# Slice attention of a four-layer graph model: softmax rows kept, turned later inside the slice mixing, and one product moved to another engine

## The chip, the cores and the metric

The kernel runs on one core of one Trainium2 chip. The core has a matrix engine (TensorE; PE in the profile, its weight loads PEld), three elementwise engines (VectorE: DVE, ScalarE: ACT, GpSimd: POOL) and a queue processor (SyncE: SP) that here mostly starts DMA transfers. Each engine takes its own instructions in the order of its queue, and waits on semaphores for the others. On-chip memory is SBUF (128 partitions); matrix products land in PSUM, which has eight banks.

The metric is the device time of the whole kernel in microseconds (us). Times are medians of several runs.

## The reference

A model of four layers works on N = 2708 nodes with D = 256 features and an adjacency matrix; each layer is a graph stage ("gnn") and a token stage ("ffn"), both with a residual. The change is in the token stage of layer 0, attention over 64 learned slices with 8 heads of 64:

```python
fx = (x @ W_fx.T + b_fx).reshape(B, N, H, P).transpose(0, 2, 1, 3)
xm = (x @ W_x.T + b_x).reshape(B, N, H, P).transpose(0, 2, 1, 3)
temp = jnp.maximum(temperature, 1e-06)
sw = jax.nn.softmax((xm @ W_slice.T + b_slice) / temp, axis=-1)
snorm = sw.sum(2)
st = jnp.einsum('bhnc,bhng->bhgc', fx, sw) / (snorm + 1e-05)[..., None]
...
ot = _hydra(st, hy_in_w, hy_conv_w, hy_conv_b, ...)
ot = ot.reshape(B, G, H, P).transpose(0, 2, 1, 3)
out = jnp.einsum('bhgc,bhng->bhnc', ot, sw).transpose(0, 2, 1, 3).reshape(B, N, D_INNER)
return out @ out_w.T + out_b
```

So every node gets, for each head, a softmax over 64 slices (512 weights in all); the weights pool the nodes into 64 slice tokens of 512 features; `_hydra`, a small state-space block run forwards and backwards, mixes the 64 tokens; and the same weights spread the result back over the nodes. The layer after it begins with `x + (concat(a @ x / deg, x) @ weight + bias)` on the layer-normed x ("L1 gnn").

## The kernel before

The 2708 rows are 22 tiles: 21 of 128 rows and a last one of 20. All is 32-bit float here. The stage has three parts, in `fast_l0_ffn`.

**The loop over the 22 tiles.** For each tile TensorE computes 512 logits (L2355: four instructions of the machine in two products of 128 input features, into `lg_ps`). VectorE adds a bias (L2367), takes the maximum per head (L2368) and subtracts it (L2369); ScalarE takes the exponential (L2372); VectorE sums per head (L2373), takes the reciprocal (L2374) and multiplies (L2375). The result `sw` (128 x 512, three buffers) then goes twice through TensorE: as the weights of the slice sums `T` (L2381, four blocks of 128 slices, accumulated over all tiles, 257 columns: the 256 normed features `fa` and a column of ones), and through four 128 x 128 transposes (L2388) into a PSUM tile that ScalarE copies (L2389) to `swT` (128 x 4 x 2708). GpSimd meanwhile adds the output bias to the residual rows (L2363, x + ob), which nothing in this loop waits for; before it, GpSimd scales an output weight of the mixing block by the norm weight (L1968, four products of 128 x 512, on data from a DMA). After the last tile, VectorE divides the sums by their weights (`Tn`).

**`Slices.mix`**, the mixing block: a long chain of small products on TensorE with elementwise work between them on the other engines, from `Tn` to `Z` (128 x 4 x 256: the mixed slices times the output projection). Its PSUM tiles a_ps to g_ps take seven banks.

**The output product.** For each tile four products of `swT` (as weights) with `Z` (L2402) and an addition to x (L2410).

The normed rows `fa`, their transposes `fT` and the projection weights lie in pools of `Pooling` that were opened before the graph stage of layer 0, in an `ExitStack` named `c0` which is closed after the ffn. What comes after is laid into the memory that becomes free then: the constants and expert weights of layer 1's routing (`Route`), and `fa`, `w`, `b` and `V` of `fast_l1_gnn`, whose front norms all rows (L1652, L1654), transposes them, projects them (L2440, into `v_ps`), splits the product into three 16-bit parts (L2451 to L2454; GpSimd makes the last) and adds the bias (L2456, GpSimd) and the own part (L2457) to x. Then comes its long loop over the adjacency matrix (L2511).

The order in each queue is not that of the source: a scheduler lays out the instructions of all engines ahead of time from its own estimates, pool by pool, so that instructions of neighbouring stages and tiles are interleaved. An instruction that reuses a buffer waits for the last reader of what lay there.

Of the kernel before, what the change touches and what calls it, by code (L numbers as in the profile page):

```python
# [18 lines left out]
N = 2708  # L19
# [1893 lines left out]
class Slices:  # L1913
# [59 lines left out]
            )  # L1973
        self.ob = ob

    def mix(self, Tn, Z):

        k, pool = self.k, self.pool
        nc, tc = k.nc, k.tc
# [3 lines left out]
        with tc.tile_pool(name="ps_b0h", bufs=1, space=PSUM) as ps, tc.tile_pool(  # L1983
# [3 lines left out]
            def psum(shape, tag):  # L1987
                return ps.tile(shape, F32, name=tag)

            def new(name, shape):  # L1990
                return sb.tile(shape, F32, name=name)


            TT = new("TT", [128, 2, DI])
            snr = new("snr", [1, DI])
            for kk in range(2):
                p_ = psum([128, DI], ("a_ps", "b_ps")[kk])
                for q in range(4):
                    nc.tensor.transpose(
                        p_[:, q * 128 : (q + 1) * 128],  # L2000
                        Tn[:, q, kk * 128 : (kk + 1) * 128],
                        ident,
                    )
                k.copy(TT[:, kk, :], p_)
            p_ = psum([1, DI], "c_ps")
            for q in range(4):
                nc.tensor.transpose(
# [21 lines left out]
            def in_proj_T(pt, c0, nch):  # L2029

                for kk in range(4):
# [5 lines left out]
                        stop=(kk == 3),  # L2037
                    )


            pd = psum([16, 64], "e_ps")
            in_proj_T(pd, 1152, 16)
# [3 lines left out]
            pb = psum([64, 2, 64], "b_ps")  # L2046
            for m in range(2):
                in_proj_T(pb[:, m, :], 2 * DI + m * 64, 64)
            t16, e16, a1, a2, dt = (new(n, [16, 64]) for n in ("t16", "e16", "a1", "a2", "dt"))
            v.tensor_scalar(t16, pd, self.dtb, None, ALU.add)  # L2050
            v.scalar_tensor_tensor(e16, t16, -1.0, t16, ALU.mult, ALU.max)
# [33 lines left out]
            xc = new("xc", [128, 6, 64])  # L2085
            nc.scalar.activation(xc, ca, AF.Silu)


            cT = new("cT", [64, 3, 16])
            pt = psum([64, 3, 16], "f_ps")  # L2090
# [5 lines left out]
            for back in range(2):  # L2096
                pr = psum([64, H, 64], ("c_ps", "d_ps")[back])
                crow = cum[:, 0:64] if back else cum[:, 1:65]
                hs = slice(back * H, (back + 1) * H)
                for h in range(H):  # L2100
                    c = back * H + h
                    nc.tensor.matmul(
                        pr[:, h, :],
                        lhsT=ident[0:16, c : c + 1].to_broadcast([16, 64]),
                        rhs=crow,
                        start=True,
                        stop=True,
                    )
                col = cT[:, 1 + back, hs, None].to_broadcast([64, H, 64])
                if back:  # L2110
                    v.tensor_tensor(E[1], col, pr, ALU.subtract)
                else:
                    v.tensor_tensor(E[0], pr, col, ALU.subtract)
                v.tensor_scalar(E[back], E[back], 0.0, None, ALU.min)
                nc.scalar.activation(E[back], E[back], AF.Exp)

            pg = psum([64, 64], "e_ps")
            nc.tensor.matmul(pg, lhsT=xc[:64, 4, :], rhs=xc[:64, 5, :], start=True, stop=True)
# [41 lines left out]
                )  # L2160
            zs = new("zs", [64, DI])
            nc.scalar.activation(zs, pz, AF.Silu)
            xr = new("xr", [64, H, P])
            pt = psum([64, DI], "a_ps")
            for q in range(4):
# [18 lines left out]
                )  # L2184
            v.tensor_tensor(y3, y3, py, ALU.add)
            v.tensor_tensor(yg, yg, zs, ALU.mult)

            ms = new("ms", [64, 1])
            nc.scalar.activation(zs, yg, AF.Square, accum_out=ms)
# [11 lines left out]
            for q in range(4):  # L2201
                for kk in range(4):
                    nc.tensor.matmul(
                        po[:, q, :],
                        lhsT=self.wo[:, kk, q * 128 : (q + 1) * 128],
                        rhs=ygT[:, kk, :],
                        start=(kk == 0),
                        stop=(kk == 3),
                    )
            bd = new("bd", [128, 4, 128])  # L2210
            nc.gpsimd.memset(bd, 0.0)
            v.tensor_copy(bd[0:64, :, 0:64], po[0:64])
# [2 lines left out]
            for s in range(2):  # L2215
                nc.tensor.matmul(
                    pm[s * 64 : s * 64 + 64],
                    lhsT=ident[:64, :64],
                    rhs=ms,
                    start=True,  # L2220
                    stop=True,
                )
            m2 = new("m2", [128, 1])
            v.tensor_copy(m2, pm)
            for q in range(4):
# [10 lines left out]
class Pooling:  # L2236
# [3 lines left out]
    def __init__(self, k, w, ctx):  # L2240
        self.k, self.w = k, w
        tc = k.tc
        H, G = 8, 64
        DI = H * G
        pool = ctx.enter_context(tc.tile_pool(name="b0a", bufs=1))
        self.tmp = ctx.enter_context(tc.tile_pool(name="b0n", bufs=2))
        self.fa = pool.tile([128, NT, D + 1], F32, name="fa")
        self.fT = pool.tile([128, 2, N], F32, name="fT")
        self.wc = pool.tile([128, 2, DI], F32, name="wc")
        self.bw = pool.tile([128, DI], F32, name="bw")  # L2250
        k.nc.gpsimd.memset(self.fa[:, :, D : D + 1], 1.0)
# [69 lines left out]
        yield  # L2321


def fast_l0_ffn(k, w, front):

# [3 lines left out]
    DI = H * P  # L2331
    with ExitStack() as ctx:
        keep = ctx.enter_context(tc.tile_pool(name="b0", bufs=1))
        swT = keep.tile([128, 4, N], F32, name="swT")
        Tn = keep.tile([128, 4, D + 1], F32, name="Tn")
        Z = keep.tile([128, 4, D], F32, name="Z")
        slices = Slices(k, w, ctx)
# [2 lines left out]
        with tc.tile_pool(name="b0t", bufs=3) as tmp:  # L2340
            with tc.tile_pool(name="ps_b0l", bufs=2, space=PSUM) as psl, tc.tile_pool(
                name="ps_b0T", bufs=1, space=PSUM
            ) as psT:

                def psum():
                    return psl.tile([128, 512], F32, name="swt_ps")

                side = front.chunk(*CHUNKS[-1], psum)
                T = [psT.tile([128, D + 1], F32, name=f"T{q}_ps") for q in range(4)]
                for t in range(NT):  # L2350
                    p = sz(t)
                    next(side, None)
                    lg = psl.tile([128, DI], F32, name="lg_ps")
                    for kk in range(2):
                        nc.tensor.matmul(  # L2355
                            lg[:p],
                            lhsT=fT[:, kk, t * 128 : t * 128 + p],
                            rhs=wc[:, kk, :],
                            start=(kk == 0),
                            stop=(kk == 1),  # L2360
                        )
                    xt = k.x[:p, t, :]
                    nc.gpsimd.tensor_tensor(xt, xt, slices.ob[:p], ALU.add)  # L2363
                    sw = tmp.tile([128, DI], F32, name="sw")
                    mx = tmp.tile([128, H], F32, name="mx")
                    s3 = sw[:p].rearrange("p (h g) -> p h g", h=H)
                    nc.vector.tensor_tensor(sw[:p], lg[:p], bw[:p], ALU.add)  # L2367
                    nc.vector.tensor_reduce(mx[:p], s3, AX.X, ALU.max)  # L2368
                    nc.vector.tensor_tensor(  # L2369
                        s3, s3, mx[:p, :, None].to_broadcast([p, H, G]), ALU.subtract  # L2370
                    )
                    nc.scalar.activation(sw[:p], sw[:p], AF.Exp)  # L2372
                    nc.vector.tensor_reduce(mx[:p], s3, AX.X, ALU.add)  # L2373
                    nc.vector.reciprocal(mx[:p], mx[:p])  # L2374
                    nc.vector.tensor_tensor(  # L2375
                        s3, s3, mx[:p, :, None].to_broadcast([p, H, G]), ALU.mult
                    )
                    tp = psum().rearrange("p (q n) -> p q n", q=4)
                    for q in range(4):
                        cols = slice(q * 128, (q + 1) * 128)  # L2380
                        nc.tensor.matmul(  # L2381
                            T[q],
                            lhsT=sw[:p, cols],
                            rhs=fa[:p, t, :],
                            start=(t == 0),
                            stop=(t == NT - 1),
                        )
                        nc.tensor.transpose(tp[:, q, :p], sw[:p, cols], ident[:p, :p])  # L2388
                    nc.scalar.copy(swT[:, :, t * 128 : t * 128 + p], tp[:, :, :p])  # L2389
                for q in range(4):  # L2390
                    sc = tmp.tile([128, 1], F32, name="sc")
                    nc.vector.tensor_scalar(sc, T[q][:, D : D + 1], 1e-5, None, ALU.add)
                    nc.vector.reciprocal(sc, sc)
                    nc.vector.tensor_scalar(Tn[:, q, :], T[q], sc, None, ALU.mult)

        slices.mix(Tn, Z)
        with tc.tile_pool(name="ps_b0o", bufs=3, space=PSUM) as ps:
            for t in range(NT):
                p = sz(t)
# [2145 lines left out]
def model(tc, I, out):  # L4545
# [4 lines left out]
    with tc.tile_pool(name="flags", bufs=1) as fp:  # L4550
# [4 lines left out]
        with ExitStack() as ctx:  # L4555
            k = Fast(ctx, tc, I["x"], bad, adjT)
            with tc.tile_pool(name="lists", bufs=1) as lp:
                edges = Edges(k, part(I, "L2_ffn_"), lp)
                with ExitStack() as c0:
# [1 line left out]
                    fast_l0_gnn(  # L4561
                        k, adjT, I["L0_gnn_WqkT"], pooling, edges.search(range(4), "right")
                    )
                    fast_l0_ffn(k, part(I, "L0_ffn_"), pooling)
                order = (0, 1, 5, 2, 3, 4)
                with ExitStack() as c1:
                    route = Route(k, c1, part(I, "L1_ffn_"), 16)
# [131 lines left out]
```

## Time and profile before

| what | value |
|---|---|
| median of 3 runs | 2408.55 us (2408.13 to 2414.51) |
| profiled execution, its own time | 2408.92 us |
| its span, first to last instruction | 2407.1 us |
| mean granted TensorE clock | 0.961 |
| softmax loop, first L2367 to last `Tn` | 372.8 to 468.6 us |
| `mix`, first transpose to first output product | 468.7 to 520.6 us |
| output product | 520.6 to 561.4 us |
| front of layer 1's graph stage | 561.4 to 613 us |

The profile is one execution. Engine rows give busy time, share of the span and number of instructions. The chain of work that ended last is, by share of the span:

```
PE 27%; DVE 3%; issue 1%; DMA 0%; POOL 0%; ACT 0%; POOLq 0%; DVEq 0%; ACTq 0%
```

In forty equal slices of the span, tenths of busy time and of the TensorE clock that was granted (the slice attention lies in slices 7 to 10, counted from one):

```
PE   7999999989899899999799999999999999969997
DVE  7588888645676558456655563234499998853544
PEclk9999999869999999999899997899999999979998
```

In all views used below, a row names the line of the kernel, the engine, the operation, and the tiles as "out<-in"; `[3.49 <-PE lg_ps L2355]` means that the engine was idle for 3.49 us before the instruction and that the PE instruction on that line ended the wait.

### The profile page before, as it was taken

What the parts mean: (1) busy time and instruction counts of PE and PEld (TensorE: products, weight loads), DVE (VectorE), ACT (ScalarE), POOL (GpSimd) and SP (SyncE); (2) the same over time, 40 slices, a digit from 0 to 9 for tenths busy, and PEclk for the clock granted to TensorE, in tenths of its full rate; (3) what the DMA queues carried; (4) which work ended last, traced back from release to release, by engine and by line L of the source; (5) the groups of instructions that cost most, each with busy time, mean ns of one, the idle gap of its engine ahead of it and who ended that gap; (6) DMA issues with size and microseconds to landing.
All of it is one profiled execution on the core that took longest, in us unless ns stands there. A gap on an engine that the chain in (4) does not pass through costs nothing. (4 is left out here: it accounts for less than half of the span.)

```text
span 2407.1 us, 31811 instructions
## 1 busy us (share of the span) xinstructions
PE 2263.5 (94%) x11620; PEld 1501.1 (62%) x11620; DVE 1530.9 (64%) x3386; ACT 687.1 (29%) x1388; POOL 454.6 (19%) x496
## 2 busy tenths in 40 slices
PE   7999999989899899999799999999999999969997
PEld 4777765577778676777578877666632333325664
DVE  7588888645676558456655563234499998853544
ACT  6433333213655222212230013233411112111121
POOL 1100013004100243565130002510030000002221
PEclk9999999869999999999899997999999999979998
DMA  5244322200756244332345523000033433314430
GB/s 150 66 114 115 113 79 79 72 4 12 236 176 188 62 116 96 82 77 48 78 135 150 146 67 59 21 1 18 1 85 101 117 108 110 92 55 160 130 123 15
DMA packets 158572, 219.99 MB, mean 91 GB/s; under 512 B 30911, under 2 KB 94115, under 8 KB 158404
## 3 DMA queue, kind: packets, MB, share of 16 engines
q1 hardware_dynamic: 126096, 179.84, 25.7%
q0 software_dynamic: 15488, 24.04, 4.9%
q10 hardware_dynamic: 16820, 13.95, 1.8%
q8 instruction: 95, 1.56, 0.3%
q14 instruction: 73, 0.60, 0.1%
HBM read 193.49 MB, written 24.82 MB: 91 GB/s over the span
## 5 line engine op out<-in xcount | busy, mean ns | idle before, releaser
L3548 DVE SCALAR_TENSOR_TENSOR PT<-Rr,Q,aj 128x512 f32<-128x512 f32 (+3 forms) x630 | 412.5, 708 | 95.8 <-PE acc_ps L3643 73.9
L3716 PE MATMUL acc_ps<-PT,V 128*64 128x512 f32 (+4 forms) x2016 | 338.9, 551 | 0.7 <-DVE PT L3548 0.2
L3716 PEld LDWEIGHTS acc_ps<-PT,V 128*64 128x64 f32 (+1 forms) x2016 | 95.3, 123 | 215.3 <-issue 163.1
L1844 PE MATMUL acc_ps<-fa,PT 128*128 128x257 f32 x882 | 215.4, 383 | 1.2 <-DVE out L1864 1.2
L1844 PEld LDWEIGHTS acc_ps<-fa,PT 128*128 128x128 f32 x882 | 163.9, 190 | 66.5 <-issue 33.8
L3643 PE MATMUL acc_ps<-V,PT 128*128 128x257 f32 x882 | 194.7, 381 | 1.0 <-POOL V L3511 0.9
L3643 PEld LDWEIGHTS acc_ps<-V,PT 128*128 128x128 f32 x882 | 166.1, 190 | 28.8 <-POOL V L3511 1.2
L3304 PE MATMUL h_ps<-xT,w1t 128*128 128x384 f32 x512 | 176.6, 498 | 3.7 <-ACT xT L3295 3.7
L3321 PE MATMUL y_ps<-w2t,hT 128*128 128x256 f32 x768 | 169.8, 380 | 0.0
L2511 PE MATMUL acc_ps<-V,at 128*128 128x257 bf16 x1323 | 157.1, 277 | 9.8 <-DVE at L2502 7.9
L3321 PEld LDWEIGHTS y_ps<-w2t,hT 128*128 128x128 f32 x768 | 144.9, 190 | 21.1
L2511 PEld LDWEIGHTS <-at 128*128 128x128 bf16 x1323 | 129.0, 99 | 32.9 <-DVE at L2502 5.5
L3304 PEld LDWEIGHTS h_ps<-xT,w1t 128*128 128x128 f32 x512 | 95.6, 192 | 67.9 <-ACT xT L3295 8.3
L1816 ACT ACTIVATE PT<-s_ps,rq 128x512 f32<-128x512 f32 (+1 forms) x126 | 79.5, 636 | 174.4 <-PE s_ps L1792 168.8
L3333 POOL DMA_INDIRECT acc<-ys,ids x48 | 92.0, 1916 | 154.1 <-DVE ys L3330 145.3
L4064 PE MATMUL y_ps<-w2t,hT 128*128 128x256 f32 (+1 forms) x528 | 119.9, 379 | 0.3 <-ACT hT L4057 0.3
L1792 PE MATMUL s_ps<-KT,QT 128*128 128x512 f32 (+1 forms) x252 | 116.2, 548 | 2.5 <-ACT PT L1816 1.6
L4050 PE MATMUL h_ps<-fT,w1t 128*128 128x512 f32 (+1 forms) x288 | 116.0, 552 | 1.9 <-PEq L4110 1.9
L3003 POOL DMA_INDIRECT xe<-fd,idg x48 | 79.6, 1659 | 195.1 <-DVE early_f L3034 180.8
L1817 DVE SCALAR_TENSOR_TENSOR PT<-aj,PT 128x512 f32<-128x512 int32 (+1 forms) x126 | 79.2, 633 | 57.9 <-ACT PT L1816 57.5
L4495 PE MATMUL y_ps<-w2t,hT 128*128 128x256 f32 (+1 forms) x512 | 112.8, 380 | 0.0
L4064 PEld LDWEIGHTS y_ps<-w2t,hT 128*128 128x128 f32 (+1 forms) x528 | 97.1, 186 | 21.3 <-issue 6.9
(745 smaller groups left out, 3368.8 us busy)
## 6 DMA issues: line engine op xcount, KB each, us to landing
aj<-in_adjT SPq DMA_DIRECT2D x399, 256.0 KB, 2.8
w1t<-in_L_ffn_W SPq DMA_DIRECT2D x8, 1024.0 KB
w2t<-in_L_ffn_W SPq DMA_DIRECT2D x8, 1024.0 KB
w1t<-in_L_ffn_w SPq DMA_DIRECT2D x8, 1024.0 KB, 5.6
w2t<-in_L_ffn_w SPq DMA_DIRECT2D x8, 1024.0 KB
aj<-in_adjT SPq DMA_DIRECT2D x63, 74.0 KB, 2.1
fd<-fa ACTq DMA_DIRECT2D x9, 512.0 KB, 3.1
aj<-in_adjT SPq DMA_DIRECT2D x21, 202.0 KB, 2.4
```

Source lines behind the costliest of these rows:

```text
L1792: nc.tensor.matmul(s[:, :cs], lhsT=QT[:, j * 128 : j * 128 + 128], rhs=KT[:, c0 : c0 + cs], start=True, stop=True,)
L1844: nc.tensor.matmul(ac, lhsT=PT[:, o : o + n], rhs=fa[:, j, :], start=j == 0, stop=False)
L2511: nc.tensor.matmul(ac[:, c:], lhsT=at[:, o : o + n], rhs=V[:, j, r], start=j == 0 and q == 0, stop=False, skip_group_check=True,)
L3304: nc.tensor.matmul(hp, lhsT=w1t[:, kk, m * 128 : (m + 1) * 128], rhs=self.xT[:, kk, :], start=(kk == 0), stop=(kk == 1),)
L3321: nc.tensor.matmul(y, lhsT=self.hT[:, m, i * 128 : (i + 1) * 128], rhs=w2t[:, m, :], start=(m == 0), stop=(m == M - 1),)
L3333: add = nc.gpsimd.indirect_dma_start(out=acc, out_offset=bass.IndirectOffsetOnAxis(ap=self.ids[:, i : i + 1], axis=0), in_=ys, in_offset=None,
L3548: nc.vector.scalar_tensor_tensor(PT, R, Q, aj, ALU.max, ALU.mult)
L3643: nc.tensor.matmul(ac[:n], lhsT=PT[:, o : o + n], rhs=V[:, j, 0, :], start=(j == 0), stop=False,)
L3716: nc.tensor.matmul(w.pop("out"), **w)
L4050: nc.tensor.matmul(o[:, :cs], lhsT=w1t[:, kk, m * 128 : (m + 1) * 128], rhs=fT[:, kk, c0 : c0 + cs], start=(kk == 0), stop=(kk == 1),)
L4064: nc.tensor.matmul(y[:n], lhsT=hT[:, m, o : o + n], rhs=w2t[:, m, :], start=(m == 0), stop=(m == M - 1),)
L4495: nc.tensor.matmul(y[:n], lhsT=hT[:, m, o : o + n], rhs=w2t[:, m, :], start=(m == 0), stop=(m == M - 1),)
```

## The change

Four things are done together.

1. The softmax rows of all tiles are kept, in `sws` (128 x 22 x 512), in the pool where `swT` was. The four transposes and the copy of each tile go out of the loop.
2. The last multiply of the softmax goes from VectorE to GpSimd.
3. The pools of `Pooling` are opened on the other side of memory, and `done()`, which is `c0.close`, gives them up after the loop, before `mix`. `swT` is laid out there.
4. A generator `turn()` makes the transposes (through one PSUM bank, `swt_ps`) and the copy of one tile at a time, every third on VectorE and the others on ScalarE. `mix` advances it at nine places with `fill(n)`, 21 tiles in all; the rest is done after `mix`. The output product is as before.

```diff
-    def mix(self, Tn, Z):
+    def mix(self, Tn, Z, side):
+            def fill(n):
+                for _ in range(n):
+                    next(side, None)
...
@@ Pooling.__init__
-        pool = ctx.enter_context(tc.tile_pool(name="b0a", bufs=1))
-        self.tmp = ctx.enter_context(tc.tile_pool(name="b0n", bufs=2))
+        right = dict(side="right")
+        pool = ctx.enter_context(tc.tile_pool(name="b0a", bufs=1, **right))
+        self.tmp = ctx.enter_context(tc.tile_pool(name="b0n", bufs=2, **right))
...
@@ fast_l0_ffn
-        swT = keep.tile([128, 4, N], F32, name="swT")
+        sws = keep.tile([128, NT, DI], F32, name="sws")
...
-                    sw = tmp.tile([128, DI], F32, name="sw")
+                    sw = sws[:, t, :]
...
-                    nc.vector.tensor_tensor(
+                    nc.gpsimd.tensor_tensor(
                         s3, s3, mx[:p, :, None].to_broadcast([p, H, G]), ALU.mult
                     )
-                    tp = psum().rearrange("p (q n) -> p q n", q=4)
                     for q in range(4):
...
-                        nc.tensor.transpose(tp[:, q, :p], sw[:p, cols], ident[:p, :p])
-                    nc.scalar.copy(swT[:, :, t * 128 : t * 128 + p], tp[:, :, :p])
...
-        slices.mix(Tn, Z)
+        done()
+        late = ctx.enter_context(tc.tile_pool(name="b0s", bufs=1, side="right"))
+        swT = late.tile([128, 4, N], F32, name="swT")
+        with tc.tile_pool(name="ps_b0s", bufs=1, space=PSUM, side="right") as ps:
+            def turn():
+                for t in range(NT):
+                    p = sz(t)
+                    tp = ps.tile([128, 4, 128], F32, name="swt_ps")
+                    for q in range(4):
+                        nc.tensor.transpose(
+                            tp[:, q, :p], sws[:p, t, q * 128 : (q + 1) * 128], ident[:p, :p]
+                        )
+                    (nc.vector.tensor_copy if t % 3 == 2 else nc.scalar.copy)(
+                        swT[:, :, t * 128 : t * 128 + p], tp[:, :, :p]
+                    )
+                    yield
+            side = turn()
+            slices.mix(Tn, Z, side)
+            for _ in side:
+                pass
...
@@ model
-                    fast_l0_ffn(k, part(I, "L0_ffn_"), pooling)
+                    fast_l0_ffn(k, part(I, "L0_ffn_"), pooling, c0.close)
```

The places of `fill` in `mix`, in its order: 1 after the transposes of `Tn`, 2 after the token projection, 3 after the input projections of the state-space block, 4 after its convolution, 2 after the decay tables, 2 after the gate, 3 after the scan's output, 2 after the output weight's product, 2 after the last projection.

More of the change, by code (lines that the diff above doesn't have):

```diff
@@ L2004, in mix @@
                 k.copy(TT[:, kk, :], p_)
+            fill(1)
             p_ = psum([1, DI], "c_ps")
@@ L2038, in in_proj_T @@
                     )
+            fill(2)
             pd = psum([16, 64], "e_ps")
@@ L2048, in mix @@
                 in_proj_T(pb[:, m, :], 2 * DI + m * 64, 64)
+            fill(3)
             t16, e16, a1, a2, dt = (new(n, [16, 64]) for n in ("t16", "e16", "a1", "a2", "dt"))
@@ L2086, in mix @@
             nc.scalar.activation(xc, ca, AF.Silu)
+            fill(4)
             cT = new("cT", [64, 3, 16])
@@ L2115, in mix @@
                 nc.scalar.activation(E[back], E[back], AF.Exp)
+            fill(2)
             pg = psum([64, 64], "e_ps")
@@ L2162, in mix @@
             nc.scalar.activation(zs, pz, AF.Silu)
+            fill(2)
             xr = new("xr", [64, H, P])
@@ L2186, in mix @@
             v.tensor_tensor(yg, yg, zs, ALU.mult)
+            fill(3)
             ms = new("ms", [64, 1])
@@ L2209, in mix @@
                     )
+            fill(2)
             bd = new("bd", [128, 4, 128])
@@ L2222, in mix @@
                 )
+            fill(2)
             m2 = new("m2", [128, 1])
@@ L2321, in chunk, with fast_l0_ffn @@
         yield
-def fast_l0_ffn(k, w, front):
+def fast_l0_ffn(k, w, front, done):
     nc, tc = k.nc, k.tc
```

## The prediction, made before the changed kernel was run

> **What bounds the kernel now.** I read the page first, then the layer-0 slice attention and the head of layer 1 stretch by stretch, because outside them (before 346 us, and from the main loop of the layer-1 graph stage, L2511, at 613 us) both programs hold the same instruction order on every engine.
>
> ```profile
> PE 2263.5 (94%) x11620; PEld 1501.1 (62%) x11620; DVE 1530.9 (64%) x3386; ACT 687.1 (29%) x1388; POOL 454.6 (19%) x496
> ```
> ```profile
> 369.00:467.00 98.00, 90.78 (x358) 54.85 (x358) 82.29 (x164) 29.70 (x51) 23.73 (x28) 1.00 0.15 48
> 468.70:480.30 11.60, 11.02 (x60) 8.35 (x60) 1.28 (x4) 1.16 (x2) 0.94 (x3) 0.50 0.96 330
> 480.30:490.00 9.70, 9.67 (x56) 9.36 (x57) 2.75 (x11) 1.54 (x2) 0.00 (x0) 0.50 0.19 60
> 490.00:499.00 9.00, 8.37 (x60) 4.71 (x58) 7.37 (x24) 3.33 (x5) 0.59 (x2) 0.88 0.01 2
> 499.00:520.60 21.60, 13.77 (x65) 12.00 (x65) 7.67 (x16) 3.83 (x8) 1.42 (x1) 0.50 0.00 0
> 520.60:561.40 40.80, 40.78 (x176) 34.27 (x176) 20.23 (x61) 0.59 (x2) 0.00 (x0) 0.94 0.00 1
> 561.40:585.90 24.50, 19.54 (x93) 16.30 (x93) 17.60 (x51) 13.96 (x34) 20.89 (x32) 0.93 0.09 28
> ```
>
> The second fence is the view by windows: sum, then busy time of PE, PEld, DVE, ACT, POOL, granted clock, DMA share, GB/s. The softmax loop is row one, the mix rows two to five, the output product row six, the front of layer 1 row seven. TensorE is nearly full in all of them, and in most of the mix it runs at clock 0.50. So work added to TensorE in the mix is dear, and work taken out of the loop is worth something only if TensorE sets the loop's pace.
>
> It doesn't quite. VectorE's timeline (start, busy, then idle time before and its releaser) shows two waits, six tiles apart:
>
> ```profile
> 425.92 0.69 DVE L2367 TENSOR_TENSOR sw<-lg_ps,bw 128x512 f32<-128x512 f32 x1 [3.49 <-PE lg_ps L2355]
> 450.55 0.69 DVE L2367 TENSOR_TENSOR sw<-lg_ps,bw 128x512 f32<-128x512 f32 x1 [3.46 <-PE lg_ps L2355]
> ```
>
> Six tiles take 24.63 us, 4.105 each. TensorE's own timeline there gives its prices, as distances between starts (the durations overlap):
>
> ```profile
> 432.19 0.60 PE L2381 MATMUL T_ps<-fa,sw 128*128 128x257 f32 x2
> 432.62 0.27 PE L2388 MATMUL swt_ps<-ident,sw 128*128 128x128 f32 x1
> 432.74 0.60 PE L2381 MATMUL T_ps<-fa,sw 128*128 128x257 f32 x2
> 433.17 0.27 PE L2388 MATMUL swt_ps<-ident,sw 128*128 128x128 f32 x1
> ```
>
> Two matmuls of the slice sums .43, a transpose .11; a logits matmul is .43 in the same way. A tile needs 3.90 of TensorE (logits 4 x .43 = 1.72, sums 8 x .217 = 1.74, transposes 4 x .11 = .44) and about 3.6 of VectorE (five 128x512 operations of .68 and the reciprocal .19); the rest is the order in which the queues hold each other.
>
> **The change, part by part.** *Loop, transposes and copy out, last multiply to GpSimd.* Removed: 88 transposes (.11 warm: 9.7 us PE), 22 ACT copies (hidden in ACT's idle 70%), 22 VectorE multiplies (15 us).
>
> ```profile
> L2375 DVE TENSOR_TENSOR sw<-sw,mx x22: 673/684/1226, 378.3 to 463.8; 128x512 f32<-128x512 f32 x21, 20x512 f32<-20x512 f32 x1
> L2388 PE MATMUL swt_ps<-ident,sw x88: 177/273/328, 379.6 to 467.0; 128*128 128x128 f32 x84, 20*128 20x20 f32 x4
> L2389 ACT COPY swT<-swt_ps x22: 226/585/586, 381.6 to 467.3; 128x512 f32<-128x512 f32 x21, 128x80 f32<-128x80 f32 x1
> ```
>
> (min/median/max ns.) In the built program the tiles now come in groups of five. A replay of the new queues with these rows gives 20.0 us a group, 4.0 a tile: 22 x .105 = 2.3 us gained, no more. The multiply on GpSimd has no row. Bounds: x+ob of half the elements takes .72 to .85, the four 128x512 products of L1968 1.23 each; 1.27 to 1.59 is paid for other two-operand products of that size. I take 1.35; at one per 4 us it is covered, as is the doubling of VectorE's own multiply when GpSimd runs (.69 to 1.2).
>
> What is not covered is GpSimd's queue. Its timeline before:
>
> ```profile
> 391.00 4.93 POOL L1968 TENSOR_TENSOR w_hy_out_wT<-w_hy_out_wT,w_hy_norm_w 128x512 f32<-128x512 f32 x4 [15.88 <-DMA w_hy_norm_w<-in_L_ffn_hy_norm_w]
> 395.89 18.68 POOL L2363 TENSOR_TENSOR x<-x,ob 128x256 f32<-128x256 f32 x22
> ```
>
> Nobody waited for these. The new program's order on GpSimd is: multiplies of tiles 0 to 5, the four L1968, 19 of the 22 x+ob, then the multiply of tile 6. Multiply 5 ends near 395.2 by the replay; +4.93 gives 400.1; 19 x .79 = 15.0 (between .716 and .849 each: 13.6 to 16.1) gives 415.1; +1.35 gives 416.4. TensorE has the slice sums of tile 6 in front of the logits of tile 10, so it stands from about 403 to 416.4, and VectorE runs dry after tile 9. Without that, tile 11's logits would come at 418.1; with it the first VectorE steps of tile 11 end at 431.75 against some 420.8: a stall of 11 us. After it the granted clock falls, as it is 0.50 after the gaps of the mix: tile 6's sums and tile 10's logits (3.5 us warm) cost up to 2.5 more. Then two groups of 20.0 and a tail of 9.9 (the tail alone is 8.4 in the replay; the last sums wait 5 us and run at half clock, 1.5): the loop ends at 431.75 + 40.0 + 9.9 = 481.6 against 468.64. **+13**, between +8 (quick x+ob, no loss of clock) and +16 (every GpSimd operation at its slow row).
>
> *Mix, 21 of the 22 turned tiles put into it.* Each is four transposes (.217 at clock 0.50) and a copy (.585 on ACT, 15 times; .69 on VectorE, 7 times), through one PSUM bank, so that each waits for the copy before it. 88 x .217 = 19.1 us of TensorE. Cover is TensorE's idle time in the four mix rows: .58 + .03 + .63 + 7.83 = 9.1. Hence 10.0 on the path; the seven VectorE copies stand in its queue before steps of the chain (copy 5 before the softplus and the convolution), which is why I don't go below that although some transposes will meet the warm stretch of row four (a replay with clock as before gives 9.9, all cold 13). Tiles 20 and 21 are turned between the first output products: four and four transposes and their hand-over, 2 us (40.8 to 43 in the replay). **+12**, between +8 (half the transposes at full clock) and +16 (gaps not used).
>
> [...]
>
> *Freed memory.* The layer-1 tiles no longer lie over swT.
>
> ```profile
> 561.48 2.08 ACT L1652 ACTIVATE fa<-x,ln_sh,ln_rs 128x256 f32<-128x256 f32 x4 [22.91 <-PE o_ps L2402]
> 565.41 8.90 PE L2440 MATMUL v_ps<-w,fT 128*128 128x256 f32 x40 [0.66 <-DMA w<-in_L_gnn_weight]
> 576.28 7.13 PE L2440 MATMUL v_ps<-w,fT 128*128 128x256 f32 x24 [1.97 <-DVE r L2452]
> 585.86 1.35 PE L2440 MATMUL v_ps<-w,fT 128*128 128x256 f32 x5 [1.14 <-DVE fT L99]
> ```
>
> ACT's normalising step waited 22.91 us for the last output product; TensorE then waited for the weights and for VectorE. In the new queues norm, x+b and the loads of w and b stand earlier and run under the output product. Row seven has 24.50 - 19.54 = 4.96 of idle TensorE; that goes, and so does the lost clock (0.93 to 1.00, some .6): **-5.5**, between -3 (only the first tile's waits go) and -8. Two moves could eat it: the set-up of the layer-1 routing (two memsets, eight small DMAs, iotas: 346.92 to 353.74, 6.8 us, hidden then) now stands on GpSimd before the first V of layer 1, and the routing weights' loads (the 0.96 DMA share of row two) move on SP from the loop's end to behind the last output product. The first V is due 7.1 us after the front starts, so 6.8 just fits; if not, some 3 us come back, which is the -3. The loads take 11 us at that share and must only be there after 613.
>
> **Sum.** +13 +12 -5.5 = +19.5 on 2408.92, the profiled execution's own time (span 2407.1 and 1.8 around it), which lies 0.4 above the median of the runs: 2428.4. About 0.3% (7.2 us) is what a measurement of this kernel can tell from no change: 2401.3 to 2415.8.
>
> **Rivals.** *One, not slower: the transposes keep TensorE at full clock through the mix.* For: the only long cold gap (7.83 us, row five) would be filled. Against: rows two and three were full and cold. Price: the cold busy time of rows two, three and five, 34.5, halves (-17.2), half the saving on the transposes counts (-4.8): -22 in place of nothing, mix and product -10. 13 - 10 - 5.5 = -2.5: 2406.4, and with the loop at +8, 2401. It decides as soon as the granted clock of the mix is above about .8.
>
> *Two: GpSimd's multiplies aren't held* (the 19 x+ob run far quicker than their .716, or the multiply of tile 6 isn't needed where I put it). Then the loop gives -1 to -2: -2 + 12 - 5.5 = +4.5, 2413.4, within the bound. Against: the order stands in the queue, and L1968 can't start before its weight lands at 391.0.
>
> *Three: worse.* The mix stays cold throughout and the single bank's hand-overs don't fit the gaps (+15), the loop takes +16, the front gives 5: 2435.
>
> **How the numbers follow.** Forecast .64, rival one .09, two .12, three .15. The forecast's own range is 2420 to 2435. The range 2412 to 2439 leaves out rival one, a third of rival two and .05 above. Faster by over 0.3%: the better half of rival one, .04. Within: the rest of it, most of rival two and a tail of the forecast, .16. Slower: .80.
>
> **What would show it.** The loop: an idle TensorE of 11 to 14 us before the sums of tile 6, put down to GpSimd's multiply, and the last Tn near 481. The mix: 62 to 65 us from its first instruction to the first output product, clock mostly 0.50 as before. The front: ACT's norm without the 22.91, and the L2440 group that starts at 585.86 now, 24.4 after the last output product, some 19 after it. It is wrong if multiply 6 starts before 405, or if the mix's windows show a clock near 1.

## The result, and the profile after

The changed kernel takes 2419.68 us (median of 7 runs, 2414.62 to 2424.34) against 2408.13 us for the kernel before (7 runs): the ratio is 1.0045, with a 95% interval of 1.003 to 1.006, so it is slower by about 11.5 us. Its profiled execution took 2424.05 us (span 2422.2) and lies at the upper end of its runs. In the changed kernel the lines are: logits L2370, bias L2382, last multiply L2390 (GpSimd), slice sums L2395, turned tiles L2418 with their copy L2421, output product L2435, projection of layer 1 L2473, its main loop L2544.

The next table cuts the two profiled executions, in us, at the first mix transpose, at the first output product, at the end of the product and at the start of layer 1's main loop. That start is the loop's first product, at 616.45 us before (L2511) and at 626.85 us after; at the 613 us of the table of before the last projection of the front has ended.

| stretch | before | after | difference |
|---|---|---|---|
| to the first step of the mix | 468.7 | 474.9 | +6.2 |
| mix | 51.9 | 61.4 | +9.5 |
| output product | 40.8 | 39.4 | -1.4 |
| front of layer 1 | 55.1 | 51.1 | -4.0 |
| from layer 1's main loop to the end | 1790.6 | 1795.4 | +4.8 |

The last row holds the same instructions in the same order on every engine in both kernels; it is taken up after the experiments.

The windows of the changed kernel, columns as in the windows of before: first the loop, then the mix, cut where the granted clock changes, then the output product.

```profile
369.00:471.60 102.60, 81.21 (x264) 50.08 (x264) 64.84 (x135) 17.59 (x29) 46.02 (x50) 0.92 0.14 46
...
474.90:479.70 4.80, 4.77 (x23) 4.00 (x24) 0.85 (x3) 1.74 (x3) 0.94 (x3) 0.50 0.00 0
479.70:483.10 3.40, 3.40 (x33) 2.58 (x31) 0.00 (x0) 0.58 (x1) 0.00 (x0) 0.99 0.00 0
483.10:500.30 17.20, 17.20 (x86) 13.75 (x84) 7.17 (x24) 0.84 (x2) 0.00 (x0) 0.50 0.00 1
500.30:507.10 6.80, 6.80 (x52) 3.90 (x51) 3.24 (x9) 4.87 (x7) 0.00 (x0) 1.00 0.00 0
507.10:534.30 27.20, 24.50 (x119) 20.49 (x120) 10.94 (x22) 7.71 (x14) 2.04 (x3) 0.50 0.00 1
...
536.30:575.70 39.40, 39.40 (x185) 33.32 (x186) 27.76 (x83) 7.67 (x17) 12.49 (x18) 1.00 0.06 18
```

In the loop TensorE has 9.6 us less to do than before and takes 4.6 us longer. In the mix it has hardly any gap left (56.7 busy of 59.4), at clock 0.50 for 49 us of it. Two things are to be noted for later: the clock changes after 3.4, 17.2, 6.8 and 27.2 us, which are 1, 5, 2 and 8 steps of about 3.4; and between 483.1 and 500.3 TensorE is busy without a break at half clock.

The loop's time went where TensorE's timeline and GpSimd's timeline show it:

```profile
412.98 3.79 PE L2395 MATMUL T_ps<-fa,sws 128*128 128x257 f32 x8 [11.28 <-POOL sws L2390]
```
```profile
393.59 4.03 POOL L1968 TENSOR_TENSOR w_hy_out_wT<-w_hy_out_wT,w_hy_norm_w 128x512 f32<-128x512 f32 x4
397.58 14.34 POOL L2378 TENSOR_TENSOR x<-x,ob 128x256 f32<-128x256 f32 x19
411.89 1.04 POOL L2390 TENSOR_TENSOR sws<-sws,mx 128x512 f32<-128x512 f32 x1
...
577.95 0.32 POOL L2962 MEMSET zero<- 128x264 f32 x1
...
584.41 0.32 POOL L2976 IOTA spare<- 128x48 f32 x1
...
584.73 0.64 POOL L2487 TENSOR_TENSOR V<-r,V 128x256 bf16<-128x256 f32 x1
```

The multiply of tile 6 starts at 411.89, behind four products and 19 additions that nobody waits for, and TensorE stands idle for 11.28 us until it is done. In return the later tiles go quicker, as VectorE's timeline shows where it showed 24.63 us for six tiles before:

```profile
428.01 0.69 DVE L2382 TENSOR_TENSOR sws<-lg_ps,bw 128x512 f32<-128x512 f32 x1 [4.37 <-PE lg_ps L2370]
446.40 0.69 DVE L2382 TENSOR_TENSOR sws<-lg_ps,bw 128x512 f32<-128x512 f32 x1 [4.14 <-PE lg_ps L2370]
```

Five tiles in 18.39 us are 3.68 a tile, against 4.105. The last rows of GpSimd's timeline belong to the front of layer 1: the routing's set-up (577.95 to 584.7) stands in front of the first V (584.73).

### The profile page after: what moved, and what is told of

The parts are those of the page before. It is cut to its first block, busy times and chain, and to the rows that moved or that the text cites. A ratio compares the mean times of both kernels' runs of the same rounds, so it can differ in the third digit from the quotient of the medians.

```text
span 2422.2 us, 31807 instructions
## 1 busy us (share of the span) xinstructions
PE 2273.1 (94%) x11620; PEld 1508.7 (62%) x11620; DVE 1519.3 (63%) x3371; ACT 684.0 (28%) x1381; POOL 478.7 (20%) x518
## 5 line engine op out<-in xcount | busy, mean ns | idle before, releaser
L2544 PE MATMUL acc_ps<-V,at 128*128 128x257 bf16 x1323 | 158.3, 279 | 10.0 <-DVE at L2535 6.2
L2544 PEld LDWEIGHTS <-at 128*128 128x128 bf16 x1323 | 129.8, 100 | 33.6 <-issue 5.2
```

Of the source, the lines that this page charges most:

```text
L2544: nc.tensor.matmul(ac[:, c:], lhsT=at[:, o : o + n], rhs=V[:, j, r], start=j == 0 and q == 0, stop=False, skip_group_check=True,)
```

## The experiments

All are read from their own profile by the same stretches; totals are medians beside the kernel before on the same chip, which gave 2410.1 to 2410.4 in these sessions.

**1. The multiply back on VectorE** (`e1_vector_mul`).

```diff
-                    nc.gpsimd.tensor_tensor(
+                    nc.vector.tensor_tensor(
                         s3, s3, mx[:p, :, None].to_broadcast([p, H, G]), ALU.mult
                     )
```

> The changed kernel with the softmax's last multiply back on VectorE, all else kept. Theory Q (place in GpSimd's queue): the 11.28 us in which TensorE waited for the multiply of tile 6 go, and with them the stretch at granted clock 0.50 after it (tile 6's sums and tile 10's logits took 6.2 us in place of some 3.6). Back comes a VectorE operation of .68 per tile; a tile needs 3.6 of VectorE and 3.46 of TensorE then, so the pace stays between 3.7 and 3.9 a tile. Mix starts near 464 (474.9 with the change, 468.7 before); mix 61, product 39, front 51 as with the change. Total some 2409 (2406 to 2413). Rival P (the wait was only a shift: VectorE is what the loop is bound by once the transposes are out): the pace goes to 4.1 or more, mix starts at 470 or later, total 2414 or more.

Measured: 2400.36 us, ratio 0.9962 (0.9945 to 0.9979): faster than the kernel before. The mix starts at 460.0, 14.9 earlier than with the change and 8.7 earlier than before. This is beyond what theory Q gave (2406 to 2413), and against rival P: VectorE runs almost without a gap at 3.2 to 3.6 us a tile. And the mix took 53.1 us, not 61, although TensorE's order in it is that of the changed kernel, instruction for instruction. Its windows say why:

```profile
460.00:463.50 3.50, 3.50 (x17) 2.81 (x18) 0.73 (x2) 1.17 (x2) 0.85 (x3) 0.52 0.02 5
463.50:484.10 20.60, 20.60 (x176) 14.98 (x175) 10.31 (x33) 7.07 (x11) 0.00 (x0) 1.00 0.00 1
484.10:511.30 27.20, 24.50 (x120) 20.51 (x118) 10.95 (x22) 7.82 (x15) 2.04 (x3) 0.50 0.00 1
```

The first part runs at full clock for 20.6 us here; with the change it had 3.4 and then 6.8. The last part, 27.2 us at 0.50, is the same to the tenth.

**2. The multiply on GpSimd, the bias additions after the loop** (`e2_ob_after_loop`).

```diff
-                    xt = k.x[:p, t, :]
-                    nc.gpsimd.tensor_tensor(xt, xt, slices.ob[:p], ALU.add)
...
+        ob = keep.tile([128, D], F32, name="ob_late")
+        nc.vector.scalar_tensor_tensor(ob, Tn[:, 0, :D], 0.0, slices.ob, ALU.mult, ALU.add)
+        for t in range(NT):
+            xt = k.x[: sz(t), t, :]
+            nc.gpsimd.tensor_tensor(xt, xt, ob[: sz(t)], ALU.add)
         done()
```

> The changed kernel, multiply still on GpSimd; the 22 additions of the output bias to the residual rows are tied to Tn (by one more VectorE operation, bias + 0 x Tn), so that GpSimd does them after the loop and not before the multiply of tile 6. L1968 stays where it was (4.0 us). Theory Q: no wait over 2 us at tile 6, pace 3.7 a tile as in the later groups of the changed kernel (18.4 for five), mix starts near 462 to 464; the 22 additions (16.6 us) run under the first part of the mix, whose first GpSimd result is needed only 25 us after its start. Total some 2408 (2405 to 2412). Rival P2 (the dear thing is a multiply on GpSimd itself, 1.04 to 1.37 us where VectorE needs .68, and the slower VectorE beside it): the loop stays as long as with the change, mix starts at 472 or later, total 2417 or more.

Measured: 2403.71 us, ratio 0.9978 (0.9964 to 0.9992); the mix starts at 462.9 and takes 53.6. In the view of waits (total, times, longest) TensorE's line for the slice sums was `19.6, 6, 11.3` with the change, and is now:

```profile
PE T_ps L2393 <- POOL sws L2388: 9.0, 6, 5.0
```

The 11.3 is gone; the longest that is left is that of the last tile. Theory Q holds and P2 falls: the place in the queue costs 12 us (474.9 against 462.9), and having the multiply on GpSimd at all some 3 more (462.9 against 460.0). Without the wait the granted clock stays at 1.00 until 457.1.

**3. Only the multiply on GpSimd, on the kernel before** (`e3_gpsimd_mul_only`). The one-word diff of experiment 1 the other way round, at L2375 of the kernel before.

> The kernel before with one edit of the change: the last multiply on GpSimd; transposes, copy and memory as before. GpSimd's queue then has L1968 and 6 of the bias additions in front of a multiply, 8 more in front of the next, 7 more in front of the one after. Theory Q: each run of additions is a wait of TensorE (6 x .76, 8 x .76 less what was ahead), together some 4 to 8 us longer in the loop, partly won back by the pace (VectorE .68 less per tile); mix starts between 468 and 476, mix, product and front as before (52, 41, 55). Total 2408 to 2415. Rival P (VectorE's work sets the loop): the loop gets shorter by some 5, total 2403.

Measured: 2428.05 us, ratio 1.0076 (1.0058 to 1.0094); the whole change had 1.0045 (1.003 to 1.006). The mix starts at 484.6 (15.9 later than before); the mix itself takes 51.9. The direction is theory Q's, the size is not: I had counted three waits behind additions, but TensorE waited eleven times.

```profile
PE T_ps L2381 <- POOL sw L2375: 17.5, 11, 5.1
```

The three waits behind the runs of 6, 8 and 8 additions took 1.5, 4.9 and 1.7 us, and that of the last tile 5.1. The pace suffered too: later multiplies come in groups of four every 17.85 us (424.97, 442.82, 460.67), 4.46 us a tile against 4.105 before. So with the transposes still in the loop a part of the price has nothing to do with the place in the queue; every tile then passes through three engines and back to TensorE, which has that tile's sums and transposes in front of the next logits, but that this is what slows the pace is argued and not shown.

**4. Only the early release, on the kernel before** (`e4_early_release`). The pools of `Pooling` on the other side, and `done()` before `mix`; `swT`, transposes and multiply as before.

> The kernel before with one edit of the change: the pools of the pooling stage on the other side and given up before the mix; softmax, transposes and copy as before. Theory: loop 468.7, mix 52 and product 41 as before; the front of layer 1 takes 51.5 in place of 55.1, because its norm, its x + b and its weights no longer wait for the last output product. Total 2404.5 (2402 to 2406). Rival: the freed memory lies elsewhere than where layer 1's first tiles are put, or the routing's set-up takes the place of the gain: no change, 2408.

Measured: 2405.83 us, ratio 0.998 (0.9967 to 0.9994). Loop end 468.5, mix 51.8, product 40.9: as before. The front takes 48.1 in place of 55.1: a gain of 7.0, more than the change has from it. Here the routing's set-up ran on GpSimd at the mix's start (467.03 to 474.7), where it lengthened nothing, and the first V came at 565.5, 4.3 us after the output product; with the change it came 9.0 after it.

```profile
467.03 0.32 POOL L2931 MEMSET zero<- 128x264 f32 x1 [53.43 <-PE swt_ps L2389]
...
565.50 0.64 POOL L2456 TENSOR_TENSOR V<-r,V 128x256 bf16<-128x256 f32 x1 [1.14 <-ACT V L2455]
```

That is the likely place of the 3.0 us of the gain that the change does not have; no run moved the set-up alone.

**5. The change again, twice** (`e5_change_again_a`, `e5_change_again_b`), unaltered.

> The changed kernel once more, unaltered. In its first profile the mix took 61.4 us, at granted clock 1.00 for one step of 3.4 us only (479.7 to 483.1); in the run with the multiply back on VectorE, and in the one with the additions after the loop, whose orders on TensorE from the first step of the mix on are the same, it took 53.1 and 53.6, with 20.5 us at 1.00. Theory C (the clock goes up or down on a grid of 3.41 us that has nothing to do with the program; which products fall into one step decides): the same program can have either; where its first part has 1.00 for some 20 us, the mix takes 53 to 55 and the total is 2414 to 2417, else 60 to 62 and 2419 to 2425. Rival W (the multiply on GpSimd or the wait in the loop makes the mix slow): 61 again whatever the total.

> As the run before it, for a second look: theory C lets the two differ by some 8 us in the mix, and the total with it; rival W has 61 in both.

Measured: 2416.56 us with a mix of 53.2, and 2425.64 us with a mix of 58.7; the mix starts at 474.8 and 475.8, and the front ends 51.2 after the product in both. The windows of the first:

```profile
474.80:478.30 3.50, 3.50 (x16) 2.88 (x16) 0.82 (x3) 1.17 (x2) 0.91 (x3) 0.50 0.00 0
478.30:498.90 20.60, 20.60 (x175) 14.92 (x175) 10.31 (x33) 6.99 (x11) 0.00 (x0) 1.00 0.00 1
498.90:526.10 27.20, 24.50 (x120) 20.50 (x119) 10.95 (x22) 7.75 (x15) 2.04 (x3) 0.50 0.00 1
```

And of the second, up to where the full clock ends:

```profile
475.80:480.80 5.00, 4.97 (x24) 4.13 (x24) 0.85 (x3) 1.75 (x3) 0.94 (x3) 0.50 0.00 0
480.80:484.20 3.40, 3.40 (x33) 2.54 (x32) 0.00 (x0) 0.59 (x1) 0.00 (x0) 0.99 0.00 0
484.20:497.90 13.70, 13.70 (x77) 12.35 (x77) 4.24 (x16) 0.26 (x1) 0.00 (x0) 0.50 0.00 1
497.90:508.10 10.20, 10.20 (x76) 5.92 (x75) 7.39 (x24) 6.48 (x10) 0.34 (x1) 1.00 0.00 0
```

The same program has six steps of full clock in a row in the first repetition, one and then three in the second, and one and then two in its first profile. Theory C holds in this: the length of the mix follows the clock, and rival W, that the change itself makes the mix 61, falls. In three profiles of it the mix took 61.4, 53.2 and 58.7; the mix of before took 51.9, 51.9 and 51.8 in the profiles of the kernel before and of experiments 3 and 4. Five profiles have one and the same order on TensorE through the mix. Where the clock rose 3.6 us (experiment 1 and the first repetition) or 4.5 us (experiment 2) after the mix's first step, it stayed high for six steps; where it rose 4.8 us (first profile) or 5.0 us (second repetition) after it, it fell again after one. What in a step decides isn't shown.

**6. The turned tiles spread among the 64-column products** (`e7_spread`), on experiment 1: `fill(1)` after every second head, after each block of the input projection and of the output weight, and fewer elsewhere.

```diff
                 nc.tensor.matmul(
                     o, lhsT=self.bfx[:, hc], rhs=snr[:, hc], start=False, stop=True
                 )
+                fill(h % 2)
...
                 in_proj_T(pc[:, m, :], DI + m * 128, 128)
+                fill(1)
```

> The kernel with the multiply back on VectorE; the turned tiles are put elsewhere in the mix: one after every second head of the token projection, one after each block of the input projection and of the output weight, fewer where TensorE waits for the chain. Theory C: every step of 3.4 us in the token and input projections then holds a tile's four 128-column transposes among the 64-column products, so the first part of the mix keeps 1.00 in whatever phase; mix 50 to 54, no run with 60; total as with the multiply back on VectorE (2400 there), 2396 to 2402, and its spread smaller. Rival W (a transpose in front of the chain's next product costs its time): each tile put before the chain costs .43 to .87, eight more of them 4 to 7 us: mix 57 to 60, total 2404 to 2408.

Measured: 2396.58 us, ratio 0.994 (0.9923 to 0.9956); five of its six runs lie between 2392.34 and 2401.62, and the profiled one took 2409.07, with a mix of 62.2. So "no run with 60" was wrong. Its first part:

```profile
459.30:485.90 26.60, 26.60 (x140) 22.39 (x140) 6.32 (x22) 4.34 (x8) 0.83 (x3) 0.50 0.00 1
```

26.6 us without a gap, with transposes among them, all at 0.50. Spread like this, they didn't bring the clock up in this stretch. The median speaks against rival W, whose total was 2404 to 2408. What the other runs' mix looked like was not profiled.

**7. Idle products where TensorE waits** (`e8_idle_matmuls`), on experiment 1: 11 products of 128 x 512 that nobody reads, in the second part of the mix.

```diff
+            def warm(n):
+                p_ = psum([128, DI], "g_ps")
+                for _ in range(n):
+                    nc.tensor.matmul(p_, lhsT=ident, rhs=TT[:, 0, :], start=True, stop=True)
...
             nc.scalar.activation(zs, pz, AF.Silu)
             fill(2)
+            warm(3)
...
             v.tensor_tensor(xD, pt, self.Dr, ALU.add)
+            warm(3)
...
             v.tensor_tensor(yg, yg, zs, ALU.mult)
+            warm(3)
             fill(3)
...
             v.tensor_copy(ygT, pt)
+            warm(2)
```

> The kernel with the multiply back on VectorE, and 11 products of 128 x 512 that nobody reads (two instructions each, .43 us at full clock, .87 at half) in the stretch of the mix where TensorE waits for the chain, beside the turned tiles. They add work only. Theory C: the stretch that had 0.50 (27 us, 484 to 511) keeps 1.00 for a good part; the output weight's product (7.1 us at 0.50) takes 3.8, a tile .65; against that 9.5 us of idle products, half of them in waiting time: mix 47 to 53, total 2394 to 2401. Rival W (work on TensorE in the mix is paid in full): 11 x 1.73 = 19 less the 4 us of waiting, mix 63 to 68, total 2410 to 2416.

Measured: 2395.88 us, ratio 0.9941 (0.9921 to 0.9961), mix 49.0:

```profile
460.70:463.60 2.90, 2.90 (x15) 2.71 (x16) 0.70 (x2) 0.69 (x2) 0.81 (x3) 0.52 0.03 6
463.60:484.80 21.20, 21.20 (x181) 15.27 (x178) 10.43 (x34) 7.75 (x13) 0.00 (x0) 1.00 0.00 1
484.80:509.70 24.90, 24.35 (x152) 16.49 (x151) 10.94 (x23) 9.11 (x18) 2.10 (x3) 1.00 0.00 1
```

With more instructions (152 against 120) the last part is 2.3 us shorter, at full clock. All three profiles with idle products (this one and those of experiments 8 and 9) have 1.00 through the last part of the mix; all nine without them have 0.50 in most of it, for six to eight steps. This is the lowest median of the study, about 14 us under the kernel before; from experiment 1 (2400.36) and experiment 6 (2396.58) it can't be told apart.

**8. More idle products from the loop's end on** (`e9_idle_from_loop_end`), on experiment 7: three each before the sums of tiles 20 and 21, three before the mix's first transposes.

> The kernel with the multiply back on VectorE and 11 idle products in the mix, which had 1.00 from 463.6 on and 0.50 from 453.4 to 463.6 (loop's end and mix's start), with 9 more idle products: three each in front of the slice sums of tiles 20 and 21, where TensorE waits 2 us for VectorE, and three in front of the mix's first transposes (1.7 us waiting). Theory C: TensorE keeps 1.00 through the loop's end; the sums of tile 20 and 21 take 3.6 in place of 5.5, the mix's first 3 us half; against it some 3 us of idle products beyond the waits: mix starts 0 to 2 earlier, mix 46 to 48 in place of 49.0, total 1 to 5 below that kernel's (2396): 2391 to 2395. Rival W (idle products are paid): 3 to 6 above it, 2399 to 2402.

Measured: 2403.49 us, ratio 0.9976 (0.996 to 0.9991): worse by 8, the direction of rival W. The mix starts at 469.0 in place of 460.7: the scheduler put idle products in front of the last logits as well, and the clock still fell to 0.50 at 459.7. The three in front of the mix took 5.46 us at half clock. But the mix was longer too, 54.4 in place of 49.0, because its clock fell again near its start:

```profile
469.90:476.70 6.80, 6.80 (x64) 5.29 (x62) 0.69 (x1) 2.12 (x4) 0.00 (x0) 1.00 0.00 0
476.70:490.50 13.80, 13.80 (x70) 11.41 (x68) 6.28 (x22) 0.84 (x2) 0.00 (x0) 0.51 0.00 1
490.50:523.40 32.90, 32.35 (x210) 21.22 (x210) 15.18 (x35) 14.47 (x24) 2.10 (x3) 1.00 0.00 1
```

So this run does not separate the price of the added products from the luck of the clock. Idle products helped, in experiment 7, where TensorE would have waited anyway and the clock did stay up.

**9. The idle products of experiment 7 on the kernel before** (`e10_before_idle_matmuls`), with nothing of the change.

> The kernel before, with nothing of the change, and the 11 idle products of 128 x 512 in the stretch of its mix in which TensorE waits for the chain (7.83 us idle of 21.6, granted clock 0.50 from 498 on). Theory C: the clock stays at 1.00 after 498; the output weight's product takes 3.8 in place of 7.1, the last products half; the idle products (9.5 us at full clock) take the waiting time and some 2 more: mix 46 to 49 in place of 51.9, product 39 in place of 40.8, total 2403 to 2406 against 2410. Rival W: 11 x .87 to 1.73 less the waiting time is paid: mix 56 to 63, total 2414 to 2420.

Measured: 2408.5 us, ratio 0.9986 (0.9972 to 1.0): not told apart from the kernel before. In its profile the mix took 49.5 and the product 38.4, close to what theory C said (the stretch from 500.1 to the mix's end had 1.00); but the front of layer 1 took 56.9 in place of 55.1, and the rest 1794.9. The effect in the mix is seen in one profile; a gain in the total is not shown.

**From layer 1's main loop to the end** the queues are equal in all these kernels. The twelve profiles have 1790.6 (before), 1795.4, 1796.2 and 1798.7 (the change, three times), and 1789.2 to 1796.9 in the eight others. So the +4.8 of the first table is inside what equal instructions show from one execution to the next. The clock goes along with it: in the clock records of these traces the six shortest (1789.2 to 1793.0) spend 123 to 134 us of the stretch at 0.50, the six longest (1794.9 to 1798.7) 139 to 154; the profile of before has 134, the first of the change 143. Whether the change adds to it (its three are in the upper part) stays open.

## Why the prediction was right in direction and too high

The forecast was 2428.4, +19.5; measured are +11.5 by medians. The sum covers only what comes before layer 1's main loop. Up to there the three profiles of the change are 10.4, 2.0 and 8.7 us behind the profile of before, and 4.8, 5.6 and 8.0 us more lie in the rest, which the sum put at nothing because the orders are equal. So the total came as near as it did partly by luck. The parts of the sum stand thus.

- **Loop, +13 predicted, +6.2 measured** (+6.1 and +7.1 in the other two profiles). The wait is there, at tile 6, behind the operations named; its place in the queue is its cause (experiments 1 and 2), and the clock fell as feared (0.50 from 404.7 to 418.3; tile 6's sums and tile 10's logits took 6.2 us in place of 3.5). Two terms were mis-sized. The step "+1.35 gives 416.4" was 3.5 late: multiply 5 ended at 393.6 and not at 395.2, the multiply of tile 6 took 1.04, the products of L1968 4.03 in place of 4.93, the 19 additions 14.34 in place of 15.0. And "two groups of 20.0" were 18.4 and 18.7. Together that is 6.4 of the 6.8.
- **The price of the other way was misjudged.** "2.3 us gained, no more" for taking transposes and multiply out was wrong: experiment 2 has 5.8 and experiment 1 8.7 at the mix's start. The replay's 20.0 us for a group of five came out as 18.4; which of its steps was too slow was not traced.
- **Mix and product, +12 predicted, +8.1 in the first profile, about 0 in the second (53.2 and 39.3 against 51.9 and 40.8), +5.4 in the third.** The step that failed is the sum itself: work at a fixed clock minus idle time. The first profile's +9.5 agrees with "10.0 on the path" by chance. The sum also counts 88 transposes, eight of which (tiles 20 and 21) it counts again in the product's 2 us; 80 would give 8.3. "TensorE is nearly full in all of them" does not fit row five either (13.77 of 21.60). With the turned tiles in it the mix has no one length: it took 61.4, 58.7 and 53.2 us in the profiles of the change with three, four and six whole steps at 1.00. The product was 1.4 shorter where I had 2 longer: its start no longer ran at half clock (1.00 against 0.94). At full clock throughout and without the two tiles it takes 38.4 (experiment 9), so they cost 1.0.
- **The clock of the mix.** The sum took rows two and three, full and at 0.50, for what the mix would have; rival one took 1.00. I weighed one against the other as if one had to win; each held in a part of the mix, in some executions: 17.2 us of unbroken matmuls stayed at 0.50 in the first profile and 26.6 in experiment 6, and 20.6 us of unbroken matmuls ran at 1.00 in the first repetition. What decides between them was not shown.
- **Rival one** (full clock through the mix, .09) came in a part of the executions and in a part of the mix, with too high a price: at best some 20.6 us of the first part of the mix had 1.00, and the last part had 0.50 for 27.2 us (1.00 for 24.9 us with idle products in it, experiment 7). The first repetition, with such a first part, took 2416.6, not 2406. That the transposes are what keeps the clock up was not shown. **Rival two** (no wait at tile 6) did not come; where it was made (experiment 2), the total fell under the kernel before. **Rival three**'s 2435 was not seen.
- **Front, -5.5 predicted, -4.0 measured.** The norm ran under the product, as said. The routing's set-up did not "just fit": it ran from 577.95 to 584.7, and the first V came after it. Experiment 4, with the set-up earlier, shows 7.0.

## What to carry to other kernels

Before work is moved to an idle engine, read what its queue already holds: operations that nobody waits for are ready early, and the scheduler put them in front here; behind 19 of them and four products, a multiply of one microsecond cost TensorE 11. The price of a stretch that ran at half clock in one execution was not fixed here (a mix of 53.2 to 61.4 us in three profiles of one program): look where the clock changes in several executions before summing instruction times. And undo a change part by part: all of it but the multiply (transposes moved from the loop into the mix, memory given up early) was worth some 10 us (2410.35 to 2400.36, ratio 0.9962), and the multiply on GpSimd cost more than that.

## What the runs showed of the hardware

- In the clock records of the kernel before and of the change's first profile, every whole stretch at one granted clock lasts a multiple of 3.413 us, from one (3.4) to 132 (450.6). Where such a step falls in the program differed between executions of the change: in the mix the clock rose 4.8, 3.6 and 5.0 us after the first step, and its stretches from there were 3.4, 17.2, 6.8 and 27.2 us in the first profile, 20.6 and 27.2 in the first repetition.
- 17.2 us of unbroken work, mostly products with 64 columns, stayed at 0.50 in the first profile of the change. Once the clock was at 1.00, it stayed there through such products for some 20.5 us in three of the five profiles with one order (experiments 1 and 2, first repetition) and fell after one step of 3.4 us in the other two. With products of 128 x 512 in the gaps, the last part of the mix had 1.00 for 24.9 us (experiment 7), where it had 0.50 for 27.2 without them (experiment 1).
- The multiply of 128 x 512 took 1.04 us on GpSimd where VectorE was idle or at a reduction (L2383, L2388), and 1.37 where VectorE's subtraction (L2384) ran beside it; that subtraction took up to 1.18 beside GpSimd's additions (L2378) where it took .69 with GpSimd idle.
